# A fused convolution, attention and expert kernel: roots moved from GpSimd to VectorE, stores made steps of SyncE's order, PSUM banks shared out anew

## The chip, the cores and the metric

The kernel runs on one core of one Trainium2 chip. The metric is the device time of one execution in microseconds. The core's engines run their own instruction streams in order: TensorE (PE in the profile), VectorE (DVE), ScalarE (ACT), GpSimd (POOL) and SyncE (SP), which only issues DMAs here. An instruction whose inputs are not ready holds up everything behind it on its engine.

## The reference, cut to what matters

The input `x` is 32 images of 128 channels by 56 by 56 pixels, float32. Two layers are applied.

```python
# layer 0: 3x3 convolution of signs, with a residual
x = x + conv(sign(group_norm(x)), sign(w)) * Alpha
# layer 1: tokens, one per pixel (3136 per image, 128 wide)
t = tokens(x)
n = layer_norm(t)
q, k, v = n @ Wq + bq, n @ Wk + bk, n @ Wv + bv
t = t + q * sum_over_tokens(k * v)
# experts: each token goes to its best 2 of 8
n = layer_norm(t)
p = softmax(n @ router_w + router_b)
top_p, top_i = top_k(p, 2);  top_p = top_p / sum(top_p)
t = t + sum_k top_p[k] * (n @ expert_w[top_i[k]] + expert_b[top_i[k]])
```

`w` is made of M, Z and rv; only its sign is used. Each layer norm needs a reciprocal square root per token, `1/sqrt(var + eps)`, and so two per token in all.

## The kernel before, in words

An image is a tile `x` of 128 channels by 3136 pixels. Its tokens are 25 chunks of up to 128 rows. The work of an image runs through these stages:

- **Convolution.** `conv` makes nine bfloat16 matmuls for eight rows of the image into a PSUM bank (tag `mm`, line 534). `conv_add` on VectorE adds them to x. `to_tokens` turns chunks (tag `tr`).
- **First norm.** VectorE takes statistics per chunk (line 574), `var1` makes 25 variances per partition (lines 443 to 446), and `rstd1` makes their reciprocal roots `r1`. ScalarE scales the tokens by r1 (`scaled`, line 625), and TensorE makes their Gram matrix (`gram`, line 634), from which the eight `kv_` steps derive the sum over k times v. `project` and `project_out` (lines 749 and 763) form q and the router's inputs. `project_add` adds them to the tokens and takes the second statistics.
- **Second norm and routing.** `var2` and `rstd2` make `r2`. `route_1` (lines 836 to 838) to `route_5` on VectorE find the two experts of each token and their gates.
- **Dense experts.** For the first 12 chunks of images 0 to 27, and for all 25 of images 28 to 31, every expert is computed. `gate_turn`, `gate_out` and `gate_parts` turn the gates and store them in DRAM (`gp`, `gb`). `spread` loads them back broadcast over partitions (`bc` and `gt`). `gated` multiplies tokens with the gates of two experts on VectorE (line 1010), and `experts` accumulates eight experts' products of a block of 512 tokens in one PSUM bank (tag `ff`, lines 1022 and 1028). `finish` adds the sum to the tokens (line 1039) and issues the store to the output (line 1040).
- **Sorted experts.** The other 13 chunks of images 0 to 27 are sorted by their pair of experts. The images form groups of 8, 8, 8 and 4. `pair_of`, `places` and `row_numbers` find where each token goes. `row_add` and `scatter` write its row to `rows` in DRAM by an indirect DMA on GpSimd (line 1201), 13 per image. When a group is complete, `list_1` to `list_4` make a list of tiles of 128 rows with one pair each. `tile_load` reads four tiles (a quad) from DRAM (`t_in`), `tile_turn` and `tile_turned` transpose them, `tile_experts` multiplies two tiles at a time with their two experts (tag `to`, line 1476), `tile_first` and `tile_second` weigh and add the products (ScalarE line 1491, VectorE line 1503). `tile_out` adds the tokens (line 1518) and stores the quad into `res` (line 1520). There are 116 quads. `result_rows` computes each token's row in `res` (`res_no`, line 1266), and `gather` fetches 13 chunks per image back by indirect DMAs (line 1271, tile `back`). `back_turn` and `back_out` turn and copy them, and the store to the output follows (line 1295).

**What sets the order.** The whole program is first a list of steps. `at` gives each step a due time, an engine, an estimate of its work in microseconds, the steps that it comes after, rings of buffers that it takes or frees, and a `delay` between the end of its work and the time when others may use what it made. `in_order` (line 94) is a planner: it plays the engines through with these estimates and picks, among the steps that can start within `AHEAD` of the earliest, the one that is due first. The order that it finds is the order in which the instructions are issued; the estimates change nothing else. `ROOM` holds the number of buffers in each ring as the planner counts them, and the `bufs` of the tile pools are those that exist. A step's `do` may issue instructions on several engines. In the kernel before, stores are issued inside steps of VectorE or ScalarE (`finish`, `tile_out`, `back_out`, `gate_out`, `gate_parts`); the DMA then stands in SyncE's queue at the place of that step, and the planner doesn't count it as SyncE's work.

**GpSimd's queue.** All scatters and gathers are issued there, at most two under way at a time (`in_turn`, `IN_FLIGHT`). The reciprocal roots stand in the same queue: `rstd_of` (line 449) raises the 25 variances per partition to the power −0.5 in one GpSimd instruction at line 450, 64 times in all. The planner counts it as 4.5 us with a delay of 3.0 (rstd1) or 6.0 us (rstd2).

**PSUM.** There are eight banks: `mm` 2, `tr` 2, `acc` 1, `ff` 1 and `to` 2. The bank `to` also serves `places`, `list_sum` and `list_3`.

Of the kernel before, what the change touches and what calls it, by code (L numbers as in the profile page):

```python
# [54 lines left out]
C = 128  # L55
# [3 lines left out]
N_EXP = 8  # L59
# [10 lines left out]
GROUPS = (8, 8, 8, 4)  # L70
IN_FLIGHT = 2
TILE_PACE = (0.7, 0.6, 0.4, 0.3)
# [9 lines left out]
    x=3, tok=3, mm=2, tr=2, acc=1, ff=1, to=2, y=3, qs=3, tt=4, bc=4, gt=2, gated=2,  # L82
    t_in=3, turned=2, v=3, back=6, sent=2,
# [13 lines left out]
def in_order(steps):  # L97
# [29 lines left out]
    while len(order) < len(steps):  # L127
# [19 lines left out]
        for f in followers.get(s.key, []):  # L147
            missing[f.key] -= 1
            same = f.engine == s.engine
            f.ready = max(f.ready, clock[s.engine] if same else s.done + HOP[f.engine])  # L150
            if not missing[f.key]:
                waiting.setdefault(f.engine, []).append(f)
# [4 lines left out]
def conv_attn_moe_kernel(  # L157
# [56 lines left out]
    ps_ff = ctx.enter_context(tc.tile_pool(name="ps_ff", bufs=1, space=PSUM))  # L214
    ps_to = ctx.enter_context(tc.tile_pool(name="ps_to", bufs=2, space=PSUM))
# [8 lines left out]
    m_half = const.tile([C, 1], F32, name="m_half")  # L224
    nc.vector.memset(m_half, -0.5)
# [223 lines left out]
    def rstd_of(var, dst):  # L449
        nc.gpsimd.tensor_tensor(dst, var, m_half.to_broadcast([C, n_ck]), ALU.pow)  # L450
# [4 lines left out]
    def plan_image(i: int):  # L455
# [160 lines left out]
        at(s + 44, ("rstd1", i), "POOL", 4.5, rstd1, after=[("var1", i)], delay=3.0)  # L616
# [289 lines left out]
        def gate_out():  # L906
# [12 lines left out]
            nc.scalar.copy(d["parts"][:, :, 0, :], d["gt"])  # L919
            gp = dpool.tile([n_gb, N_EXP, WIDE], F32, tag="gp", name=f"gp_{i}")  # L920
            nc.sync.dma_start(
                gp.rearrange("(h b) e (c t) -> (b e c) h t", h=per_j, c=PER), sb[:rows]
# [3 lines left out]
        def gate_parts():  # L926
# [6 lines left out]
            nc.vector.tensor_sub(parts[:, :, 2, :], rem, parts[:, :, 1, :])  # L933
            gb = dpool.tile([n_db, 3, N_EXP, WIDE], BF16, tag="gb", name=f"gb_{i}")
# [17 lines left out]
        at(s + 119, ("rstd2", i), "POOL", 4.5, rstd2, after=[("var2", i)], delay=6.0)  # L952
# [15 lines left out]
            after=[("gate_turn", i), ("gate_parts", i - 1), ("spread", i - 2, n_units - 1)],  # L968
            delay=3.0,
# [3 lines left out]
            after=[("gate_out", i)], free=[("tr", ("gate_turn", i))], delay=4.0,  # L973
# [62 lines left out]
        def finish(b):  # L1036
            lo, hi = cols_of(b)
            t = d.pop(("tt", b))[:, : hi - lo]
            nc.vector.tensor_add(t, t, d.pop(("ff", b))[:, : hi - lo])
# [3 lines left out]
        last_unit = (last_dense(i - 1) + 1) * pairs - 1  # L1043
# [599 lines left out]
```

## Time and profile before

| | |
|---|---|
| device time, median of 3 runs | 3037.72 us (3020.0 to 3044.76) |
| the profiled execution | 3027.72 us |
| its span, first to last instruction | 3026.0 us |
| mean granted TensorE clock | 0.879 |
| TensorE busy | 2332.3 us (77%) |
| VectorE busy | 1975.5 us (65%) |
| ScalarE busy | 1352.9 us (45%) |
| GpSimd busy | 1151.2 us (38%), of which the 64 roots 281.9, the 364 scatters 445.3 and the 364 gathers 414.4 |
| DMA | 467.06 MB, 154 GB/s on average |

A profile page lists busy time per engine, groups of instructions by source line, and waits: `A <- B: sum, times, longest` is the idle time of engine A just before an instruction, ended by the named instruction of B. A timeline row gives start, duration, engine, line, operation, output and input, how many instructions the row merges, and in brackets the idle time before it and what ended it. A view of stretches gives the busy time of each engine between two times; PEclk is the TensorE clock that was granted, as a share of full speed. The scatters of images 0 to 13 are issued before the first gather at 1084.0 us, those of images 14 to 27 after it; the last scatter is issued at 2510.7 us and the last gather at 3018.9 us.

### The profile page before, as it was taken

The page shows a single profiled execution, that of the slowest core. Times are in us where ns is not written, and L with a number is a line of the kernel's source. Part 1 is how long each engine was busy: PE and PEld are TensorE (multiplying, and loading weights), DVE is VectorE, ACT ScalarE, POOL GpSimd, SP SyncE. Part 2 cuts the span into 40 slices and gives each one's busy share as a digit, 9 for nine tenths or more (in the row PEclk, how much of TensorE's full clock was granted, in tenths as well). Part 3 has the DMA queues.
Part 4 walks back from the last instruction along what each step waited for, and adds up shares of the span by engine and source line. Part 5 has one row for each costly group of instructions (what it writes and reads, how often), then busy time and mean ns, then how long its engine had stood idle before and what let it go on. Part 6 is the DMA issues. An engine that isn't in the chain of part 4 may idle for free. (4 is left out here: it accounts for less than half of the span.)

```text
span 3026.0 us, 43562 instructions
## 1 busy us (share of the span) xinstructions
PE 2332.3 (77%) x11990; PEld 1535.9 (51%) x11990; DVE 1975.5 (65%) x5998; ACT 1352.9 (45%) x4211; POOL 1151.2 (38%) x908
## 2 busy tenths in 40 slices
PE   5887978798888986677678767767686687869767
PEld 3654545455666654354455444545464454645533
DVE  3867867687777876576566656557565574657644
ACT  5545544455555554344544443434444443432310
POOL 1244333333332344423343345443433433234443
PEclk9888989899999998898889888888797798979878
DMA  3343444355555544463545344334664464746556
GB/s 128 98 148 132 163 132 135 133 176 177 168 174 162 180 147 144 122 191 120 163 145 176 116 140 156 104 123 153 185 179 116 141 177 121 232 126 225 172 186 209
DMA packets 309729, 467.06 MB, mean 154 GB/s; under 512 B 61129, under 2 KB 209009, under 8 KB 309490
## 3 DMA queue, kind: packets, MB, share of 16 engines
q1 hardware_dynamic: 285186, 414.11, 43.1%
q0 software_dynamic: 23296, 46.64, 5.1%
q10 hardware_dynamic: 1008, 3.54, 0.3%
q8 instruction: 100, 1.64, 0.2%
q14 instruction: 139, 1.14, 0.1%
HBM read 345.73 MB, written 118.39 MB: 153 GB/s over the span
## 5 line engine op out<-in xcount | busy, mean ns | idle before, releaser
L1028 PE MATMUL ff<-gated,ew_d 128*128 128x512 f32 (+1 forms) x1792 | 902.8, 639 | 189.9 <-DVE gated L1010 189.7
L1201 POOL DMA_INDIRECT rows<-tok,row_no x364 | 445.3, 1223 | 882.4 <-issue 320.8
L1271 POOL DMA_INDIRECT back<-res,res_no x364 | 414.4, 1138 | 786.5 <-PE back_ps L1286 392.4
L1028 PEld LDWEIGHTS ff<-gated,ew_d 128*128 128x128 f32 x1792 | 351.5, 210 | 594.5 <-issue 341.1
L1010 DVE TENSOR_TENSOR gated<-tt,bc 128x1024 f32<-128x1024 f32 (+1 forms) x448 | 527.5, 1183 | 145.0 <-PE ff L1028 105.5
L534 PE MATMUL cv<-xs,w_bin 128*128 128x448 bf16 x2016 | 437.1, 363 | 35.4 <-ACT xs L500 18.6
L625 ACT ACTIVATE y<-tok,r 128x128 f32<-128x128 f32 (+1 forms) x800 | 256.5, 396 | 397.2 <-POOL r L450 374.5
L450 POOL TENSOR_TENSOR r<-var,m_half 128x25 f32<-128x25 f32 x64 | 281.9, 4410 | 199.1 <-DVE var L446 183.0
L763 ACT ACTIVATE qs<-q,r 128x136 f32<-128x136 f32 (+1 forms) x800 | 244.2, 386 | 206.1 <-PE q L749 175.9
L1476 PE MATMUL to<-ew_s,turned 128*128 x1856 | 265.2, 290 | 85.2 <-ACT turned L1464 39.8
L534 PEld LDWEIGHTS <-w_bin 128*128 128x128 bf16 x2016 | 199.9, 100 | 220.9 <-issue 74.4
L1476 PEld LDWEIGHTS to<-ew_s,turned 128*128 128x128 f32 x1856 | 243.6, 202 | 123.6 <-ACT turned L1464 58.2
L749 PE MATMUL q<-move,x 128*128 128x144 f32 (+1 forms) x1600 | 261.5, 304 | 22.6 <-ACT qs L767 11.1
L749 PEld LDWEIGHTS q<-move,x 128*128 128x128 f32 (+1 forms) x1600 | 230.0, 200 | 70.8 <-issue 34.6
L1491 ACT ACTIVATE v<-to,t_in 128x128 f32<-128x128 f32 x464 | 186.0, 457 | 174.3 <-PE to L1476 145.0
L634 PE MATMUL gram<-y 128*128 128x129 f32 (+1 forms) x1600 | 218.7, 286 | 39.8 <-ACT y L625 39.6
L634 PEld LDWEIGHTS gram<-y 128*128 128x128 f32 (+1 forms) x1600 | 205.3, 199 | 73.0 <-ACT y L625 45.1
L1503 DVE SCALAR_TENSOR_TENSOR v<-to,t_in,v 128x128 f32<-128x128 f32 x464 | 139.4, 343 | 126.6 <-ACT v L1491 108.9
L574 DVE BATCH_NORM_STATS2 st<-tok 128x6 f32<-128x128 f32 (+1 forms) x800 | 177.6, 276 | 24.8 <-ACT tok L567 23.7
L775 DVE TENSOR_TENSOR tok<-tok,qs 128x384 f32<-128x384 f32 (+1 forms) x288 | 148.6, 516 | 58.4 <-ACT qs L763 33.4
L782 DVE BATCH_NORM_STATS2 st<-tok 128x6 f32<-128x128 f32 (+1 forms) x800 | 181.5, 276 | 0.0
L545 DVE SCALAR_TENSOR_TENSOR x<-cv,alpha_col,x 128x448 f32<-128x448 f32 x224 | 151.0, 675 | 42.8 <-PE cv L534 36.7
(208 smaller groups left out, 2733.0 us busy)
## 6 DMA issues: line engine op xcount, KB each, us to landing
bc<-gp SPq DMA_DIRECT2D x432, 512.0 KB
x<-in_x_dram SPq DMA_DIRECT2D x64, 784.0 KB
t_in<-rows SPq DMA_DIRECT2D x464, 66.0 KB
res<-v SPq DMA_DIRECT2D x116, 256.0 KB
out_dram<-tt SPq DMA_DIRECT2D x108, 256.0 KB
out_dram<-o SPq DMA_DIRECT2D x84, 256.0 KB
gt<-gb SPq DMA_DIRECT2D x324, 24.0 KB
rows<-zeros SPq DMA_DIRECT2D x116, 66.0 KB
```

What stands on the lines that cost most here:

```text
L450: nc.gpsimd.tensor_tensor(dst, var, m_half.to_broadcast([C, n_ck]), ALU.pow)
L534: nc.tensor.matmul(cv, lhsT=w_bin[:, t, :], rhs=xs[:, b * ROWS + dy : b * ROWS + dy + ROWS, dx : dx + width], start=(t == 0), stop=(t == T ...
L625: nc.scalar.mul(y[:n, j, :C], d["tok"][:n, c, :C], d["r1"][:n, c : c + 1])
L634: nc.tensor.matmul(d["gram"], lhsT=y[:n, j, :C], rhs=y[:n, j, :], start=(c == 0), stop=(c == n_ck - 1),)
L749: nc.tensor.matmul(p[:n, k, :], lhsT=d["x"][:, c * C : c * C + n], rhs=move, start=True, stop=True,)
L763: nc.scalar.mul(qs[:n, k, : C + N_EXP], p[:n, k, : C + N_EXP], d["r1"][:n, c : c + 1])
L1010: nc.vector.tensor_tensor(g[:, :, :n], d["tt", b][:, :n].unsqueeze(1).to_broadcast([C, 2, n]), d.pop(("bc", b, k))[:, :, :n], ALU.mult,)
L1028: nc.tensor.matmul(d["ff", b][:, :n], lhsT=ew_d[:, e * C : (e + 1) * C], rhs=g[:, j, :n], start=False, stop=(e == N_EXP - 1),)
L1201: dma = nc.gpsimd.indirect_dma_start(out=groups[group]["rows"], out_offset=bass.IndirectOffsetOnAxis(ap=d["row_no"][:n, c - N_DENSE : c - ...
L1271: dma = nc.gpsimd.indirect_dma_start(out=d["back", c][:n, :], out_offset=None, in_=groups[group]["res"][: quads_of(group) * WIDE, :], in_o ...
L1476: nc.tensor.matmul(p[:, k, j, :], lhsT=t[:, n * C : (n + 1) * C], rhs=ew_s[:, bass.ds(d["cols", q][j][n], C)], start=True, stop=True,)
L1491: nc.scalar.activation(d["v", q][:, 2 * h + k, :], d["to", q, h][:, k, 0, :], AF.Identity, bias=row[:, C + 2 : C + 3], scale=row[:, C : C ...
```

## The change

It has four parts.

1. **Roots.** `rstd_of` no longer uses GpSimd. VectorE makes a first guess from the bits of the variance (a shift right by one and a subtraction from 0x5F3759DF, both on int32) and improves it in three Newton steps of three instructions each: 11 instructions on 25 columns in place of one. The steps rstd1 and rstd2 become VectorE steps of 1.25 us without delay.
2. **Stores.** The stores inside `finish`, `tile_out`, `back_out`, `gate_out` and `gate_parts` become steps of SyncE of their own (`store`, `tile_store`, `back_store`, `gate_store`, `parts_store`), with places in SyncE's order, work and landing times. The buffers that they read are freed by them. `spread`, `tile_load`, `pad` and `gather` get larger estimates of work or landing time, and a step on the same engine as one with a delay now waits in the plan for the landing, unless it is of the same kind. `gather` comes after `tile_store`, and `spread` after `gate_store`.
3. **Buffers.** The row numbers `row_no` and `res_no` get four buffers instead of two, and `result_rows` of an image comes after the gathers of the image three before it, instead of two. `back` gets eight buffers instead of six, while the planner still counts six.
4. **PSUM.** `ff` gets two banks and `to` one.

```diff
 ROOM = dict(
-    x=3, tok=3, mm=2, tr=2, acc=1, ff=1, to=2, y=3, qs=3, tt=4, bc=4, gt=2, gated=2,
-    t_in=3, turned=2, v=3, back=6, sent=2,
+    x=3, tok=3, mm=2, tr=2, acc=1, ff=2, to=1, y=3, qs=3, tt=4, bc=4, gt=2, gated=2,
+    t_in=3, turned=2, v=3, back=6, sent=2, o=2,
 )
...
+GATE_LANDS, SPREAD_LANDS, STORE_LANDS, TILE_LANDS, GATHER_LANDS = 5.0, 6.5, 5.0, 6.0, 6.0
...
-            same = f.engine == s.engine
+            same = f.engine == s.engine and (not s.delay or f.key[0] == s.key[0])
...
-    ps_ff = ctx.enter_context(tc.tile_pool(name="ps_ff", bufs=1, space=PSUM))
-    ps_to = ctx.enter_context(tc.tile_pool(name="ps_to", bufs=2, space=PSUM))
+    ps_ff = ctx.enter_context(tc.tile_pool(name="ps_ff", bufs=2, space=PSUM))
+    ps_to = ctx.enter_context(tc.tile_pool(name="ps_to", bufs=1, space=PSUM))
...
     def rstd_of(var, dst):
-        nc.gpsimd.tensor_tensor(dst, var, m_half.to_broadcast([C, n_ck]), ALU.pow)
+        square = spool.tile([C, n_ck], F32, tag="square", bufs=1, name="square")
+        shape = [C, n_ck]
+        nc.vector.tensor_tensor(
+            square.bitcast(I32),
+            var.bitcast(I32),
+            one_i.to_broadcast(shape),
+            ALU.logical_shift_right,
+        )
+        nc.vector.tensor_tensor(
+            dst.bitcast(I32), guess.to_broadcast(shape), square.bitcast(I32), ALU.subtract
+        )
+        for _ in range(NEWTON):
+            nc.vector.tensor_mul(square, dst, dst)
+            nc.vector.scalar_tensor_tensor(square, square, -0.5, var, ALU.mult, ALU.mult)
+            nc.vector.scalar_tensor_tensor(dst, square, 1.5, dst, ALU.add, ALU.mult)
...
-        at(s + 44, ("rstd1", i), "POOL", 4.5, rstd1, after=[("var1", i)], delay=3.0)
+        at(s + 44, ("rstd1", i), "DVE", 1.25, rstd1, after=[("var1", i)])
...
-        at(s + 119, ("rstd2", i), "POOL", 4.5, rstd2, after=[("var2", i)], delay=6.0)
+        at(s + 119, ("rstd2", i), "DVE", 1.25, rstd2, after=[("var2", i)])
...
+        at(
+            s + 138, ("gate_store", i), "SP", 0.4, gate_store,
+            after=[("gate_out", i), ("spread", i - 2, last_units(i - 2))], delay=GATE_LANDS,
+        )
...
+        at(
+            s + 139, ("parts_store", i), "SP", 0.35 * n_db, parts_store,
+            after=[("gate_parts", i), ("spread", i - 2, last_units(i - 2))], delay=GATE_LANDS,
+        )
...
-                    begin + n * unit - 12, ("spread", i, n), "SP", 0.1 + 0.3 * (k == 0), spread, b, k,
-                    after=[("gate_out", i), ("spread", i, n - 1), ("spread", i - 1, last_unit)]
-                    + ([("gate_parts", i)] if k == 0 else []),
-                    take=["bc"] if k else ["bc", "gt"], delay=4.5,
+                    begin + n * unit - 12, ("spread", i, n), "SP", 0.35 + 1.0 * (k == 0), spread, b, k,
+                    after=[("gate_store", i), ("spread", i, n - 1), ("spread", i - 1, last_unit)]
+                    + ([("parts_store", i)] if k == 0 else []),
+                    take=["bc"] if k else ["bc", "gt"], delay=SPREAD_LANDS,
...
-                free=[("ff", ("experts", i, b * pairs)), ("tt", ("tt_turn", i, b))],
+                free=[("ff", ("experts", i, b * pairs))],
+            )
+            at(
+                begin + n * unit + 5, ("store", i, b), "SP", 0.35, store, b,
+                after=[("finish", i, b)], free=[("tt", ("tt_turn", i, b))], delay=STORE_LANDS,
             )
...
-            d["res_no"] = spool.tile([C, n_sort], U32, tag="res_no", bufs=2, name=f"res_no_{i}")
+            d["res_no"] = spool.tile([C, n_sort], U32, tag="res_no", bufs=4, name=f"res_no_{i}")
...
-            d["back", c] = bpool.tile([C, C], F32, tag="back", bufs=6, name=f"back_{i}_{c}")
+            d["back", c] = bpool.tile([C, C], F32, tag="back", bufs=8, name=f"back_{i}_{c}")
...
-            after=[("list_2", group), ("gather", i - 2, n_ck - 1), ("result_rows", i - 1)],
+            after=[("list_2", group), ("gather", i - 3, n_ck - 1), ("result_rows", i - 1)],
+            delay=3.0,
...
-                    + [("tile_out", group, q) for q in range(quads_of(group))],
-                    take=["back"], delay=3.0,
+                    + [("tile_store", group, q) for q in range(quads_of(group))],
+                    take=["back"], delay=GATHER_LANDS,
...
+            at(
+                due + each * k / n_sort + 8, ("back_store", i, b), "SP", 0.35, back_store, b,
+                after=[("back_out", i, b)], free=[("o", ("back_out", i, b))], delay=STORE_LANDS,
+            )
...
+            at(
+                due + 8, ("tile_store", g, q), "SP", 0.35, tile_store, g, q,
+                after=[("tile_out", g, q), ("tile_store", g, q - 1)]
+                + ([("gather", last_of[g - 2], n_ck - 1)] if q == 0 and g > 1 else []),
+                free=[("v", ("tile_first", g, q, 0))], delay=STORE_LANDS,
             )
```

## The prediction

> **What bounds the kernel now.** I read the summary, the waits, the stages and one stretch of the timeline, in that order. The summary says that no engine is full:
>
> ```profile
> span 3026.0 us, 43562 instructions
> PE 2332.3 (77%) x11990; PEld 1535.9 (51%) x11990; DVE 1975.5 (65%) x5998; ACT 1352.9 (45%) x4211; POOL 1151.2 (38%) x908
> ```
>
> TensorE stands idle for about 690 us. The waits of all engines say what the others stood at:
>
> ```profile
> POOL back L1271 <- PE back_ps L1286: 392.4, 70, 38.9
> ACT y L625 <- POOL r L450: 374.5, 29, 30.5
> ...
> DVE logit L837 <- POOL r L450: 236.1, 28, 26.4
> ...
> DVE res_no L1266 <- DMA back<-res,res_no: 162.2, 15, 24.1
> ...
> PE ff L1022 <- DVE tt L1039: 68.4, 14, 14.4
> ...
> DVE a L1181 <- POOL r L450: 57.4, 4, 19.1
> ```
>
> Three of these are the reciprocal root on GpSimd (L450), awaited by ScalarE and VectorE for 374.5 + 236.1 + 57.4 = 668 us, though 64 of them are busy for only 282 us. The stages show when it hurts:
>
> ```profile
> 640.00:1084.00 444.00, 402.19 (x2286) 276.92 (x2285) 355.47 (x1107) 254.54 (x802) 145.22 (x89) 0.95 0.55 171
> 1084.00:1600.00 516.00, 372.85 (x1974) 246.92 (x1974) 326.04 (x1037) 236.86 (x749) 210.59 (x150) 0.85 0.48 150
> ```
>
> The columns are the stretch, its length, busy time of PE, PE loads, DVE, ACT and POOL, granted clock, DMA share and GB/s. The first gather starts at 1084.0. Before it TensorE is busy 402/444 = 91%, after it 373/516 = 72%. The timeline from 1249 on shows how; first GpSimd, then the engines that wait for it:
>
> ```profile
> 1270.29 0.95 POOL L1271 DMA_INDIRECT back<-res,res_no  x1 [0.89 <-DMA back<-res,res_no]
> 1271.68 0.95 POOL L1271 DMA_INDIRECT back<-res,res_no  x1 [0.44 <-issue]
> 1272.65 8.64 POOL L450 TENSOR_TENSOR r<-var,m_half 128x25 f32<-128x25 f32 x2
> ```
>
> ```profile
> 1257.04 0.18 DVE L446 SCALAR_TENSOR_TENSOR var<-var,diff 128x25 f32<-128x25 f32 x1
> ...
> 1277.04 0.70 ACT L625 ACTIVATE y<-tok,r 128x128 f32<-128x128 f32 x2 [26.95 <-POOL r L450]
> 1277.50 1.23 PE L634 MATMUL gram<-y 128*128 128x129 f32 x4 [17.93 <-ACT y L625]
> 1281.32 0.37 DVE L837 TENSOR_TENSOR logit<-logit,r 128x200 f32<-128x200 f32 x1 [23.79 <-POOL r L450]
> ```
>
> The variances are ready at 1257.2; GpSimd takes up the two roots at 1272.65, behind gathers and scatters queued ahead of them, and the whole core waits. Pairing each variance (L446) with its root (L450), the time from one to the other is 5.4 us on average in 640 to 1084 and 13.8 us in 1084 to 1600, at most 28.1 us. Laying TensorE's gaps over the stretches in which ScalarE or VectorE waits for r gives 347 us of TensorE idle; with VectorE's waits for an old gather (res_no) added it is 381 us, with the ff wait 401 us. This overlap, not the 668 us, is what can come back.
>
> **What the Trainium skill says.** "GPSIMD Engine Reference", section 3.1: an elementwise operation on two inputs is about twice as slow on GpSimd as on VectorE at 2048 elements. The trace agrees in direction, and more: pow over 25 columns takes 4.41 us, a VectorE operation of that shape 0.17 to 0.19 us (L443 to L446). "VectorE: DVE Perf Modes", errata section: an f32 tensor-tensor takes (N+151)/0.96 ns, so 183 ns for N = 25; L443 has 188. "TensorE: Matmul & The Clock Gate", Part 1: TensorE falls to half clock after some 3.4 us idle. The trace agrees: granted clock is 0.95 in the busy stage, 0.85 after. "Perfetto Trace Analysis", section on tensor performance: independent groups of matmuls should rotate through PSUM banks so that emptying one overlaps the next. The 68.4 us before L1022 show the lack of it for ff; the change takes the same thing from `to`.
>
> **The change, part by part.**
>
> *Roots by Newton on VectorE.* Removed: 64 × 4.41 = 282 us of GpSimd, its place in that queue and two hops between engines. Added: per root 2 + 3 × 3 = 11 instructions of 25 columns. The shift isn't in the trace; it is bounded by the shortest and longest row of that shape, 0.17 and 0.19 us, and I take 0.18 (at most 1.3 us over all 64 either way). So 11 × 0.18 = 2.0 us busy and, each depending on the last (dependent ones start 0.20 us apart at 1207.2), 2.2 us from var to r instead of 4.4 plus the queue. In sum 64 × 2.0 = 127 us more VectorE. It lies beside TensorE's work where VectorE has room (880 busy of 1426 us from 1084 to 2510, 62%), less so in 640 to 1084 (80%). Behind it on VectorE stand gated products that feed ff. I count a quarter, +32; bounds 0 and +127. The gain: of 381 us I count 70%, −267. The rest goes to what is late next: `PE back_ps <- DMA back` is 95 us now, and gathers keep their own queue. Bounds −150 and −381.
>
> *Clock.* Filling gaps warms TensorE. After 1084 it is busy 1425 us at 0.85 to 0.86; halfway to 0.95 is 0.90, and 1425 × (1 − 0.85/0.90) = 79 us. Half of that shows in the span: −40; bounds 0 and −79.
>
> *More buffers for row numbers, back 6 to 8.* The res_no wait is within the 381. `back` gets two buffers that the planner (still 6) doesn't count on; that shields GpSimd's 392 us at L1271, of which only 84 us coincide with TensorE idle. No root is behind it any more, so I count nothing; at most −84, and where the cover of other GpSimd work goes, nothing is lost either, since a buffer adds no work.
>
> *Stores as SyncE steps.* The same DMAs: 112 tt, 112 o, 116 res, 32 gp and 112 gb, about 0.35 us of issue each on SP. They are moved later in SP's order, past bc and t_in loads. SP stands long at them (L1520 257 us, L1295 97 us), but who needs the loads behind hardly waits: gated for bc 9.3 us, PE turn for t_in 8.9, ACT v 5.6. So −10, bounds −25 and +30. The loss: the tt, o and v buffers are freed by a store that now may sit behind loads, and a tile_store that comes late holds back every gather of its group. A gate_store or parts_store now delays spread by 5.0 + 0.5 us in the plan only. The dearer SP costs and landing times (spread 6.5, gather 6.0) shift order, not work.
>
> *PSUM.* ff 1 to 2: takes the 68.4 us before L1022, of which 20 are outside the 381: −20; bounds 0 and −68. `to` 2 to 1: each of 232 half tiles (L1476) must be emptied by two L1491 (2 × 0.457) and two L1503 (2 × 0.343 us), 1.6 us plus hops, before the next may start; places, list_sum and list_3 take the same bank. Now TensorE waits 29.5 us for L1503 here. The plan puts other matmuls between as long as ScalarE and VectorE keep time: a quad comes every (1080−675)/32 = 12.7 us for the first group, and two emptyings with matmuls need about 7. Cover gone, the cost is 232 × 1.6 = 371 us. I take +40; bounds 0 and +371.
>
> Sum against the profiled execution, 3027.7 us (span 3026.0 and 1.7 around it): −267 −40 −10 −20 +32 +40 = −265, so 2763. The median of the runs, 3037.7, is 0.33% above the profiled one: **2770 us**.
>
> **Rivals.**
>
> *The pace before the gathers returns (2600).* Images' scatters come 74 us apart in 640 to 1084 and about 103 apart from 1084 to 2510 (14 images). If nothing takes the root's place, the latter falls to about 78: 14 × 25 = 350 saved, and some 70 of the last 516 us: 3027.7 − 420 = 2608. For it: all the work is in both stages but 13 gathers an image. Against: those need GpSimd too.
>
> *The indirect DMAs remain the pace (2900).* From 1084 on there are 364 gathers and 182 scatters, two under way at most, now 3.56 us apart. In the last 166 us 63 go at 2.6 us with little else queued. If in the mix they only reach 3.3, 546 × 3.3 = 1802 after a start at about 1070, and 20 for the end: about 2890. For it: `POOL rows <- DMA rows` 190.8 us, and the last chain runs through gathers. Against: most of those waits have no compute behind them once the root is gone.
>
> *The single `to` bank decides (3150, slower).* If ScalarE or VectorE is behind plan, TensorE, being in order, stands at L1476, and all behind it: ff, conv, back. Gain without it is 305 us, so it decides from 305/232 = 1.3 us per half tile. At 1.9 us it costs 441: 3027.7 − 305 + 441 = 3164. For it: the planner prices L1491 at 0.70 per half where two take 0.91, and L1503 at 0.53 where two take 0.69. Against: its hops, 0.5 to 0.8 us, exceed the trace's 0.1 to 0.2, so the plan has slack.
>
> *The change does not do what it says* (the roots still late, as VectorE is itself behind gathers): about 3010.
>
> **Numbers.** 2770 (2680 to 2860): 0.50. The early pace: 0.20. The gather pace: 0.15. Within 1%: 0.04. The single bank: 0.11. Differences under 1% can't be told from none here (the three runs span 0.8%). The range of 8 in 10 goes from 2580 to 2960: it leaves out the slower case, no change, and a twentieth below. Faster by over 1% is 0.85, within 1% 0.04, slower 0.11.
>
> **What would show it.** Right: no L450 on POOL; VectorE busy some 2100 us; the waits for r gone from ACT y and DVE logit; from the first gather on TensorE over 80% busy at a clock near 0.90; `PE ff <- DVE tt` near zero; waits at L1476 below 70 us. Wrong: L1476's waits for DVE v in hundreds of microseconds (single bank); `PE back_ps <- DMA back` far above 95 us (gather pace); gated waiting for bc or tiles for t_in by far more than 9 us (stores).

## The result and the profile after

The changed kernel takes **2550.05 us** (median of 4 runs, 2532.56 to 2556.39); the kernel before, beside it, 3036.92 us. The ratio is 0.8394, 95% interval 0.8339 to 0.8448: faster by 16%. The prediction was 2770 us with a range of 2580 to 2960; the direction was right, the measured time lies 30 us below the range, and the gain is almost twice the forecast one. The profiled execution took 2551.04 us, 477 less than that of before.

The summary of the page after, span, busy times and granted clock (busy time in us, share of the span):

```profile
span 2549.3 us, 44202 instructions
PE 2244.8 (88%) x11990; PEld 1490.2 (58%) x11990; DVE 2058.0 (81%) x6703; ACT 1349.8 (53%) x4211; POOL 885.7 (35%) x844
...
PEclk9999999999999999989999999979999999999986
```

TensorE has the same 11990 matmuls. It is busy 87 us less, as its mean granted clock rose from 0.879 to 0.956, and span minus busy time fell from 693.7 to 304.5 us: 389 us of idle are gone. 389 + 87 = 476 us, the whole gain. VectorE has 705 instructions and 82.5 us more.

The waits of all engines after (sum in us, times, longest):

```profile
ACT v L1549 <- PE to L1534: 282.0, 151, 7.1
...
POOL back L1319 <- PE back_ps L1334: 152.5, 59, 12.1
...
PE back_ps L1334 <- DMA back<-res,res_no: 121.4, 53, 11.2
...
DVE gated L1050 <- PE ff L1068: 96.1, 61, 13.3
...
ACT y L650 <- DVE r L471: 44.9, 10, 10.9
...
PE to L1534 <- DVE v L1561: 40.2, 32, 2.9
...
DVE res_no L1314 <- DMA back<-res,res_no: 26.2, 6, 7.8
```

The 668 us in which ScalarE and VectorE waited for a root on GpSimd are 44.9 us, all ScalarE's. The wait for an old gather (`res_no`) went from 162.2 to 26.2, GpSimd's wait for a free `back` from 392.4 to 152.5. The wait of `ff` for VectorE's additions (68.4 before) is in no row. TensorE's largest wait before was for the gated products of VectorE, which itself stood waiting for roots:

```profile
PE ff L1028 <- DVE gated L1010: 189.7, 31, 25.3
```

The same wait (`PE ff L1068`) is 15.2 us after. What waits now is mostly ScalarE for `to`, which costs no TensorE time (the run with the old PSUM banks below).

To see where the 477 us came from, both runs are cut at the same points of the work: the first scatter of image 1, the first scatter of image 8, the first gather, the last scatter, the end. The views of stretches have the same columns as in the prediction. Before:

```profile
0.00:192.50 192.50, 134.91 (x704) 89.96 (x704) 111.50 (x392) 103.48 (x318) 46.31 (x134) 0.90 0.32 109
192.50:677.90 485.40, 403.99 (x2000) 249.12 (x1999) 360.69 (x1163) 238.96 (x788) 182.26 (x106) 0.91 0.45 150
677.90:1084.00 406.10, 368.24 (x2107) 255.12 (x2106) 328.31 (x1018) 233.83 (x735) 138.61 (x87) 0.95 0.56 170
1084.00:2510.70 1426.70, 1034.74 (x5504) 700.50 (x5504) 880.73 (x2755) 632.38 (x1961) 579.71 (x426) 0.85 0.47 147
2510.70:3026.00 515.30, 390.47 (x1684) 241.19 (x1682) 294.29 (x675) 144.30 (x411) 204.27 (x158) 0.86 0.58 184
```

After:

```profile
0.00:165.40 165.40, 124.09 (x686) 81.20 (x687) 113.68 (x439) 104.00 (x320) 26.49 (x130) 0.97 0.37 127
165.40:559.10 393.70, 384.64 (x1993) 243.74 (x1992) 380.78 (x1318) 237.52 (x783) 126.64 (x92) 1.00 0.57 184
559.10:956.40 397.30, 367.46 (x2143) 256.79 (x2141) 349.68 (x1143) 237.59 (x744) 103.27 (x79) 1.00 0.57 174
956.40:2106.60 1150.20, 1015.35 (x5627) 692.76 (x5626) 940.28 (x3144) 642.07 (x2006) 468.67 (x397) 0.95 0.61 188
2106.60:2549.30 442.70, 353.26 (x1549) 215.68 (x1547) 273.56 (x661) 128.61 (x364) 160.65 (x149) 0.89 0.65 200
```

By length the five stages gained 27, 92, 9, 277 and 73 us. The fourth, with scatters and gathers mixed, is the largest, as expected. The second is the surprise: before any gather, images 1 to 8 had 81 us of TensorE idle and have 9 now. An image took 69 us there and takes 56 (393.7/7), and VectorE is now 97% busy (380.78/393.70): it, and not TensorE alone, is full in this stage.

One root in the fourth stage, on VectorE (start, duration, line, operation; rows of VectorE alone):

```profile
1493.47 0.18 DVE L452 SCALAR_TENSOR_TENSOR var<-var,diff 128x25 f32<-128x25 f32 x1
...
1493.86 0.17 DVE L459 TENSOR_TENSOR square<-var,one_i 128x25 int32<-128x25 int32 x1
1493.94 0.28 DVE L807 BATCH_NORM_STATS2 st<-tok 128x6 f32<-128x128 f32 x1
1494.15 0.17 DVE L465 TENSOR_TENSOR r<-guess,square 128x25 int32<-128x25 int32 x1
...
1496.71 0.19 DVE L471 SCALAR_TENSOR_TENSOR r<-square,r 128x25 f32<-128x25 f32 x1
```

The root is done 3.3 us after its variance. Between its instructions stand those of other steps: within one engine the program isn't issued step by step, as the section on the kernel before says, but with independent neighbours mixed in. This matters below. Pairing all 64 variances with their roots, the time from one to the other is 5.5 us on average and 14.7 at most, where the kernel before had 10.5 and 28.1.

### The profile page after: what moved, and what is told of

The parts are those of the page before. It is cut to its first block, busy times and chain, and to the rows that moved or that the text cites. A ratio compares the mean times of both kernels' runs of the same rounds, so it can differ in the third digit from the quotient of the medians.

```text
span 2549.3 us, 44202 instructions
## 1 busy us (share of the span) xinstructions
PE 2244.8 (88%) x11990; PEld 1490.2 (58%) x11990; DVE 2058.0 (81%) x6703; ACT 1349.8 (53%) x4211; POOL 885.7 (35%) x844
## 5 line engine op out<-in xcount | busy, mean ns | idle before, releaser
L1068 PE MATMUL ff<-gated,ew_d 128*128 128x512 f32 (+1 forms) x1792 | 848.2, 599 | 15.3 <-DVE gated L1050 15.2
L1249 POOL DMA_INDIRECT rows<-tok,row_no x364 | 466.6, 1282 | 1060.4 <-DMA rows<-tok,row_no 155.9
L1319 POOL DMA_INDIRECT back<-res,res_no x364 | 409.6, 1125 | 596.4 <-PE back_ps L1334 152.5
L1068 PEld LDWEIGHTS ff<-gated,ew_d 128*128 128x128 f32 x1792 | 320.6, 196 | 271.0 <-issue 212.7
L1534 PE MATMUL to<-ew_s,turned 128*128 x1856 | 264.9, 283 | 88.0 <-DVE v L1561 40.2
L559 PEld LDWEIGHTS <-w_bin 128*128 128x128 bf16 x2016 | 199.1, 100 | 187.3 <-issue 44.9
L650 ACT ACTIVATE y<-tok,r 128x128 f32<-128x128 f32 (+1 forms) x800 | 247.2, 395 | 46.4 <-DVE r L471 44.9
L774 PE MATMUL q<-move,x 128*128 128x144 f32 (+1 forms) x1600 | 252.4, 296 | 13.8 <-DVE x L570 7.9
L774 PEld LDWEIGHTS q<-move,x 128*128 128x128 f32 (+1 forms) x1600 | 221.9, 194 | 50.8 <-issue 28.8
L659 PEld LDWEIGHTS gram<-y 128*128 128x128 f32 (+1 forms) x1600 | 213.9, 200 | 55.0 <-ACT y L650 29.6
L659 PE MATMUL gram<-y 128*128 128x129 f32 (+1 forms) x1600 | 228.5, 290 | 13.1 <-ACT y L650 12.8
L599 DVE BATCH_NORM_STATS2 st<-tok 128x6 f32<-128x128 f32 (+1 forms) x800 | 180.4, 276 | 21.9 <-ACT tok L592 21.6
L807 DVE BATCH_NORM_STATS2 st<-tok 128x6 f32<-128x128 f32 (+1 forms) x800 | 184.8, 276 | 0.0
L1334 PE MATMUL back_ps<-ident,back 128*128 128x128 f32 (+1 forms) x364 | 75.7, 299 | 123.3 <-DMA back<-res,res_no 121.4
```

The lines of the kernel that those rows point to most:

```text
L559: nc.tensor.matmul(cv, lhsT=w_bin[:, t, :], rhs=xs[:, b * ROWS + dy : b * ROWS + dy + ROWS, dx : dx + width], start=(t == 0), stop=(t == T ...
L650: nc.scalar.mul(y[:n, j, :C], d["tok"][:n, c, :C], d["r1"][:n, c : c + 1])
L659: nc.tensor.matmul(d["gram"], lhsT=y[:n, j, :C], rhs=y[:n, j, :], start=(c == 0), stop=(c == n_ck - 1),)
L774: nc.tensor.matmul(p[:n, k, :], lhsT=d["x"][:, c * C : c * C + n], rhs=move, start=True, stop=True,)
L807: nc.vector.bn_stats(st2[:n, c, :], d["tok"][:n, c, :C])
L1068: nc.tensor.matmul(d["ff", b][:, :n], lhsT=ew_d[:, e * C : (e + 1) * C], rhs=g[:, j, :n], start=False, stop=(e == N_EXP - 1),)
```

## Experiments

The theory was: the roots came late since they stood in GpSimd's queue behind scatters and gathers that wait for their turn. The rivals for the gain: the stores and estimates (a different plan), the PSUM banks, and the buffers. All runs, with medians of four executions and the ratio to the kernel before beside them (its medians lie between 3024 and 3037):

| run | median us | ratio (95%) |
|---|---|---|
| the change | 2550.05 | 0.8394 (0.8339 to 0.8448) |
| roots_alone | 2605.90 | 0.8612 (0.8593 to 0.8631) |
| roots_undone | 2998.71 | 0.9905 (0.9876 to 0.9935) |
| stores_undone | 2553.50 | 0.8452 (0.8430 to 0.8474) |
| psum_undone | 2545.78 | 0.8396 (0.8355 to 0.8437) |
| bufs_undone | 2629.40 | 0.8671 (0.8624 to 0.8718) |
| roots_bufs | 2564.81 | 0.8464 (0.8421 to 0.8507) |
| roots_old_plan | 2714.48 | 0.8964 (0.8917 to 0.9012) |
| before_flight4 | 2863.21 | 0.9482 (0.9436 to 0.9527) |
| newton8 | 2708.57 | 0.8944 (0.8902 to 0.8986) |
| spare15 | 2553.81 | 0.8468 (0.8426 to 0.8510) |
| newton2 | 2537.65 | 0.8391 (0.8356 to 0.8426) |
| in_flight4 | 2428.11 | 0.8025 (0.7987 to 0.8063) |
| flight3 | 2534.15 | 0.8376 (0.8341 to 0.8412) |
| flight8 | 2622.58 | 0.8662 (0.8603 to 0.8721) |
| flight4_newton2 | 2586.73 | 0.8567 (0.8535 to 0.8599) |
| flight4_spare15 | 2655.28 | 0.8743 (0.8690 to 0.8796) |

### Which part does it

**The roots alone, in the kernel before.**

```diff
-        nc.gpsimd.tensor_tensor(dst, var, m_half.to_broadcast([C, n_ck]), ALU.pow)
+        # the 11 VectorE instructions of the change
...
-        at(s + 44, ("rstd1", i), "POOL", 4.5, rstd1, after=[("var1", i)], delay=3.0)
+        at(s + 44, ("rstd1", i), "DVE", 1.25, rstd1, after=[("var1", i)])
...
-        at(s + 119, ("rstd2", i), "POOL", 4.5, rstd2, after=[("var2", i)], delay=6.0)
+        at(s + 119, ("rstd2", i), "DVE", 1.25, rstd2, after=[("var2", i)])
```

> The kernel before with one part of the change: the roots by Newton steps on VectorE, stores, buffers and PSUM as before. Theory (the root behind gathers and scatters in GpSimd's queue is the cost): most of the 487 us come, 2630 to 2750 us. Rival 1 (the stores in SyncE's order and the dearer landing times made the plan true to the chip, and that is the gain): little, 2900 to 3000 us. Rival 2 (PSUM: two ff banks): 2900 to 3000 us as well, with the wait of ff for DVE tt still tens of us.

It gains 418 us of the 487, with nothing else of the change in it.

**The change with its roots back on GpSimd** (the same lines the other way round).

> The changed kernel with the roots back on GpSimd as one power instruction, 4.5 us with delays of 3.0 and 6.0 in the plan, all else as changed. Theory: 2850 to 3000 us, with the waits of ACT y and DVE logit for r back at several hundred us. Rival 1 (stores and estimates): stays near the changed kernel, 2560 to 2700 us. Rival 2 (PSUM): the same, 2560 to 2700 us.

Three parts without the roots gain 1%. Its waits show the roots as late as ever, 722 us against 668 in the kernel before, and the single bank holding TensorE (`PE to`, 128 us) once ScalarE and VectorE fall behind:

```profile
ACT y L632 <- POOL r L453: 383.3, 31, 29.7
...
DVE logit L844 <- POOL r L453: 288.5, 29, 30.0
...
PE to L1516 <- DVE v L1543: 128.1, 41, 22.1
...
DVE a L1211 <- POOL r L453: 50.6, 3, 19.8
```

**The stores and estimates of before, with roots, buffers and banks of the change.** The edit is part 2 of the diff, taken out:

```diff
-            at(
-                begin + n * unit + 5, ("store", i, b), "SP", 0.35, store, b,
-                after=[("finish", i, b)], free=[("tt", ("tt_turn", i, b))], delay=STORE_LANDS,
-            )
...
```

> The changed kernel with the stores back inside the steps that make their data and the old estimates of work and landing, with Newton roots, buffers and PSUM as changed. Theory: a small loss, 2560 to 2640 us, since those who need loads hardly waited for them. Rival 1: most of the gain goes, 2800 us or more, with SyncE standing at stores and gated products waiting for bc.

2553.5 against 2550.1 us: the intervals of the two ratios overlap. The stores and estimates are worth nothing that can be told apart, in either direction.

**The PSUM banks of before.**

```diff
-    x=3, tok=3, mm=2, tr=2, acc=1, ff=2, to=1, y=3, qs=3, tt=4, bc=4, gt=2, gated=2,
+    x=3, tok=3, mm=2, tr=2, acc=1, ff=1, to=2, y=3, qs=3, tt=4, bc=4, gt=2, gated=2,
...
-    ps_ff = ctx.enter_context(tc.tile_pool(name="ps_ff", bufs=2, space=PSUM))
-    ps_to = ctx.enter_context(tc.tile_pool(name="ps_to", bufs=1, space=PSUM))
+    ps_ff = ctx.enter_context(tc.tile_pool(name="ps_ff", bufs=1, space=PSUM))
+    ps_to = ctx.enter_context(tc.tile_pool(name="ps_to", bufs=2, space=PSUM))
```

> The changed kernel with one ff bank and two to banks, all else as changed. Theory: within 40 us of the changed kernel either way, 2520 to 2590 us: the ff wait of 68 us comes back in part, and the waits at the to matmuls (88 us) go in part. Rival 2: most of the gain goes, 2700 us or more.

2545.8 us: nothing either, for the two banks together; the run doesn't part a gain by `ff` from a loss by `to`. With the second bank back, ScalarE's wait for `to` falls from 282 to 115 us and the time stays, so that wait wasn't on the path.

**The buffers of before, in the changed kernel.**

```diff
-            d["row_no"] = spool.tile([C, n_sort], U32, tag="row_no", bufs=4, name=f"row_no_{i}")
+            d["row_no"] = spool.tile([C, n_sort], U32, tag="row_no", bufs=2, name=f"row_no_{i}")
...
-            d["res_no"] = spool.tile([C, n_sort], U32, tag="res_no", bufs=4, name=f"res_no_{i}")
+            d["res_no"] = spool.tile([C, n_sort], U32, tag="res_no", bufs=2, name=f"res_no_{i}")
...
-            d["back", c] = bpool.tile([C, C], F32, tag="back", bufs=8, name=f"back_{i}_{c}")
+            d["back", c] = bpool.tile([C, C], F32, tag="back", bufs=6, name=f"back_{i}_{c}")
...
-            after=[("list_2", group), ("gather", i - 3, n_ck - 1), ("result_rows", i - 1)],
+            after=[("list_2", group), ("gather", i - 2, n_ck - 1), ("result_rows", i - 1)],
```

> The changed kernel with two buffers for row_no and res_no, six for back, and result_rows after the gathers of the image two before. The roots alone stand at 2606 us, the whole at 2550; stores undone and PSUM undone each left it at about 2550. If the buffers carry the rest: 2580 to 2620 us, with the wait of res_no for DMA back at 100 us or more. If the rest is shared by overlapping parts: 2540 to 2575 us.

79 us slower than the change. VectorE's wait for `res_no` is 76.6 us again (26.2), GpSimd's for `back` 286.3 (152.5), TensorE's for VectorE at `to` 77.6 (40.2). Which of the three sizes does it, or the image that `result_rows` waits for, wasn't separated.

**Roots and buffers alone, in the kernel before** (the two edits above together).

> The kernel before with two parts of the change, the roots and the buffers; stores and PSUM as before. If these two are the whole gain: 2530 to 2575 us. If stores and PSUM, which each may stand in for the other, carry something together: 2580 to 2610 us.

2564.8 us: the buffers add 41 to the roots' 418, and what is left for stores and banks together is some 15 us, not told apart from none. So the two undoings (449 and 79) and the two additions (418 and 41) agree in kind: roots first, buffers second, nothing else that can be told apart.

### Why the root's place costs so much

**Only the root's instructions changed, the plan left as it was.** The planner goes on treating rstd1 and rstd2 as GpSimd's work of 4.5 us with 3 or 6 us of delay; only the body of `rstd_of` is new.

```diff
-        nc.gpsimd.tensor_tensor(dst, var, m_half.to_broadcast([C, n_ck]), ALU.pow)
+        # the 11 VectorE instructions of the change; both at(...) as before
```

> The kernel before with only the instructions of the root replaced by Newton on VectorE; the plan still counts the roots as GpSimd steps of 4.5 us with delays of 3.0 and 6.0, so that every step stands where it stood before. Theory A (the chip's own GpSimd queue made the roots late): nearly as fast as the kernel with the roots moved in the plan too (2606 us), 2600 to 2720 us. Theory B (the plan, which made room for a slow root, was what cost): most of the 418 us stay, 2850 to 3020 us.

313 us of the gain come with the plan untouched, so from what happens on the chip. Another 109 come when the plan knows it (2714 to 2606). In this run the roots cost ScalarE 99 us, and the wait for `res_no` is as long as before:

```profile
DVE res_no L1284 <- DMA back<-res,res_no: 181.6, 17, 24.0
...
ACT y L643 <- DVE r L468: 99.2, 17, 14.5
```

There is a rival here. In the kernel before, GpSimd also stood 183.0 us for variances (`POOL r L450 <- DVE var L446`) and was busy 282 us with the roots, and the gathers behind it had to wait; without roots in its queue they could come sooner, and that could be the gain. But TensorE's wait for gathered rows was too short for that, and it didn't fall. Before, and then in this run:

```profile
PE back_ps L1286 <- DMA back<-res,res_no: 95.4, 39, 10.0
```

```profile
PE back_ps L1304 <- DMA back<-res,res_no: 143.7, 56, 11.1
```

The wait for `res_no` rose too (162.2 before). What fell is the part of TensorE's idle time that coincides with waits for r: laid over each other as in the prediction, 347 us before, 34 here, 9 with the roots alone and 8 in the changed kernel. So it is the wait for the root, and not the gathers behind it, that carries the 313 us.

**Four indirect DMAs under way in the kernel before,** its roots still on GpSimd, so that its queue drains sooner:

```diff
-IN_FLIGHT = 2
+IN_FLIGHT = 4
```

> The kernel before with four indirect DMAs under way instead of two, roots still on GpSimd, all else as before. Theory (the roots stand behind gathers and scatters that wait for a DMA two before them): GpSimd's queue drains sooner, the roots come sooner, 2750 to 2930 us, with the waits of ACT y and DVE logit for r well below 668 us. If the roots are late for other reasons, such as gathers waiting for a free back buffer: 2950 to 3030 us.

161 us faster by a constant alone. From variance to root it is 6.1 us on average now (10.5 with two), and the waits for r are 352 us in place of 668:

```profile
ACT y L625 <- POOL r L450: 179.3, 27, 19.9
DVE logit L837 <- POOL r L450: 159.4, 28, 15.5
...
DVE a L1181 <- POOL r L450: 13.1, 2, 9.2
```

This speaks for the queue theory without touching the root, and GpSimd is as busy with the roots as before. TensorE's idle time that coincides with waits for r fell from 347 to 138 us. It isn't pure: gathers also come sooner (`PE back_ps` waits 33.3 us for them, 95 before).

**Eight Newton steps in place of three,** 15 more instructions in a chain; the plan still counts 1.25 us.

```diff
-NEWTON = 3
+NEWTON = 8
```

> The changed kernel with eight Newton steps instead of three, the plan unaware of it: 26 instructions, some 5.2 us from variance to root, more than the 4.4 us of the power on GpSimd, and 64 x 15 x 0.18 = 173 us more VectorE. Theory A (the wait in the queue, not the duration of the root): 2590 to 2700 us, the added VectorE work showing by a quarter to three quarters. Rival C (the root's duration on the path): 64 x 3 us = 190 us or more on top of the added work, 2740 us or more.

158.5 us slower than the change. VectorE's busy time rose by 143.5 us to 2201.5, which looks like the price. The next run tests that.

**The same 15 instructions, on nobody's path.**

```diff
         for _ in range(NEWTON):
...
+        spare = spool.tile([C, n_ck], F32, tag="spare", bufs=1, name="spare")
+        for _ in range(5):
+            nc.vector.tensor_mul(spare, var, var)
+            nc.vector.scalar_tensor_tensor(spare, spare, -0.5, var, ALU.mult, ALU.mult)
+            nc.vector.scalar_tensor_tensor(spare, spare, 1.5, spare, ALU.add, ALU.mult)
```

> The changed kernel with 15 more VectorE instructions of 25 columns behind each root, whose result nobody reads, the plan unaware: the added work of eight Newton steps without the longer way from variance to root for ScalarE. Eight steps cost 158 us. If VectorE's busy time is what they cost: 2680 to 2730 us, as with eight steps. If the longer way to the root (15 x 0.2 = 3 us, 64 times) is: 2550 to 2620 us.

2553.8 us: 960 more instructions cost nothing that can be told apart. The timeline shows where they go:

```profile
204.77 0.18 DVE L469 TENSOR_TENSOR square<-r 128x25 f32<-128x25 f32 x1
204.87 0.18 DVE L474 TENSOR_TENSOR spare<-var 128x25 f32<-128x25 f32 x1
204.99 0.19 DVE L470 SCALAR_TENSOR_TENSOR square<-square,var 128x25 f32<-128x25 f32 x1
205.09 0.18 DVE L475 SCALAR_TENSOR_TENSOR spare<-spare,var 128x25 f32<-128x25 f32 x1
205.21 0.19 DVE L471 SCALAR_TENSOR_TENSOR r<-square,r 128x25 f32<-128x25 f32 x1
```

L469, L470 and L471 depend on each other and start 0.22 us apart; a spare one fits between two of them. In the changed kernel the same chain stands alone, at the same pace:

```profile
205.55 0.19 DVE L469 TENSOR_TENSOR square<-r 128x25 f32<-128x25 f32 x1
205.77 0.18 DVE L470 SCALAR_TENSOR_TENSOR square<-square,var 128x25 f32<-128x25 f32 x1
205.99 0.19 DVE L471 SCALAR_TENSOR_TENSOR r<-square,r 128x25 f32<-128x25 f32 x1
```

So newton8's loss doesn't come from the number of VectorE's instructions. It isn't shown that busy time is free, though: a stretch in which two instructions overlap counts once, and so the spare ones added 59.6 us of busy time where the chain added 143.5. The summaries of newton8 and then of spare15 (2058.0 us of VectorE in the change):

```profile
PE 2323.2 (86%) x11990; PEld 1533.3 (57%) x11990; DVE 2201.5 (81%) x7663; ACT 1363.9 (50%) x4211; POOL 904.4 (33%) x844
```

```profile
PE 2244.7 (88%) x11990; PEld 1489.6 (58%) x11990; DVE 2117.6 (83%) x7663; ACT 1351.5 (53%) x4211; POOL 886.4 (35%) x844
```

From variance to root it takes 15.3 us on average in newton8 (5.9 with the spare ones), and ScalarE waits 100.6 us for r (44.9 in the change). But TensorE doesn't stand idle in those waits: they coincide with its idle time for 7 us, against 8 in the change. Its idle time as a whole grew by 82 us, and its waits for results of VectorE from 119 to 203 us; the other 78 us are its busy time, at a granted clock of 0.932 in place of 0.956. So the chain seems to cost by holding up VectorE's own stream, and with it what TensorE awaits from there, and not by ScalarE's wait for r. No run separates the two.

This also corrects the theory. 15.3 us is more than the 10.5 of the kernel before, which took 3037 us and not 2709. How late a root is doesn't give its cost; what the other engines stand for it does: newton8's chain lies in VectorE's own stream, with other work mixed in, and its r is awaited for 100.6 us; GpSimd's root came late behind waits for DMAs and was awaited for 668.

**Two Newton steps.**

```diff
-NEWTON = 3
+NEWTON = 2
```

> The changed kernel with two Newton steps, a root that is exact to some 5e-6 only: eight dependent instructions where the change has eleven. Five steps more cost 158 us, 10.5 us for each instruction added to the chain (64 roots). If the chain of the root is exposed on both sides of three steps: 3 x 10.5 = 32 us less than 2550, 2505 to 2530 us. If it is exposed only where it is long: 2540 to 2560 us. If the order of the program that comes out by chance outweighs it: outside both, above 2560 us.

2537.7 us, 12 less (ratio 0.8391 against 0.8394: not told apart). At its present length the chain costs nothing that can be told apart.

### What bounds it next

**Four under way in the changed kernel** (the `IN_FLIGHT` edit above).

> The changed kernel with four indirect DMAs under way instead of two. If the gathers' pace still bounds the end (PE back_ps waits 121 us for DMA back, the last 200 us have TensorE at 70%): 2450 to 2520 us. If the pace is set by GpSimd's own work or by the DMA engines: within 1% of 2550 us.

2428.1 us, 122 less than the change and 20% less than the kernel before: **the version that beats both**. TensorE is busy 91% of the span at a clock of 0.976, and it hardly waits for gathers any more (121.4 before this edit):

```profile
span 2422.7 us, 44157 instructions
PE 2216.3 (91%) x11990; PEld 1479.2 (61%) x11990; DVE 2056.7 (85%) x6703; ACT 1347.8 (56%) x4211; POOL 907.2 (37%) x844
```

```profile
PE back_ps L1334 <- DMA back<-res,res_no: 30.3, 23, 8.0
```

The gain lies after the first gather, as the theory of the gathers' pace has it: from there to the end it takes 1465.6 us in place of 1592.9, and up to there the same as the change to within 1 us.

**Three, and eight.**

```diff
-IN_FLIGHT = 2
+IN_FLIGHT = 3
```

> The changed kernel with three indirect DMAs under way. If the pace of the gathers bounds the end and eases in step with the number: 2450 to 2510 us. If the number matters little and four hit a lucky order: 2530 to 2560 us.

> The changed kernel with eight indirect DMAs under way. Four took it to 2428 us, with PE back_ps waiting 30 us for DMA back. More should bring little: 2400 to 2430 us; above 2440 us if the DMAs take one another's engines.

Three give 2534.2 us, not told apart from two (their intervals overlap), and eight 2622.6, slower than two. More isn't better, and the miss at eight raises the question whether four holds up when something small beside it changes.

**Four with two Newton steps, and four with the spare instructions,** each edit worth nothing that can be told apart by itself.

> The changed kernel with four indirect DMAs under way and two Newton steps instead of three, so a root that is exact to some 5e-6 only. If VectorE's added work shows nearly in full, as with eight steps: 64 x 3 x 0.165 = 32 us less than the 2428 us of four under way, 2385 to 2410 us. If VectorE has room again: 2415 to 2435 us.

> The changed kernel with four indirect DMAs under way and 15 spare VectorE instructions behind each root, three Newton steps. At two under way the spare ones cost nothing. If four under way hold a gain of 120 us whatever the exact order: 2415 to 2450 us. If the 2587 us with two Newton steps show that the gain hangs on the order that came out: anywhere up to 2620 us, with engines idle after the first group's lists for no releaser that the profile shows.

2586.7 and 2655.3 us: both lose the whole gain of four and more. Their traces show waits of a kind that the change and in_flight4 don't have. Of flight4_newton2, all engines:

```profile
731.16 0.96 POOL L1249 DMA_INDIRECT rows<-tok,row_no  x1 [0.30 <-issue]
731.35 0.59 ACT L592 COPY tok<-xt 128x512 f32<-128x512 f32 x1 [2.72 <-remote]
...
731.99 0.67 PE L586 MATMUL xt<-ident,x 128*128 128x128 f32 x4 [3.11 <-issue]
...
735.24 0.96 POOL L1249 DMA_INDIRECT rows<-tok,row_no  x1 [0.30 <-DMA rows<-tok,row_no]
736.37 0.59 ACT L1030 COPY tt<-l 128x512 f32<-128x512 f32 x1 [4.43 <-remote]
736.50 0.96 POOL L1249 DMA_INDIRECT rows<-tok,row_no  x1 [0.30 <-DMA rows<-tok,row_no]
737.01 1.11 PE L1516 MATMUL turn<-ident,t_in 128*128 128x128 f32 x4 [4.36 <-issue]
```

GpSimd issues scatters back to back, one each 1.26 us, and TensorE and ScalarE stand for 3 to 4 us at a time with no releaser among the core's instructions ("remote", "issue"); the matmuls at L1023 that ScalarE's L1030 reads had ended at 727.2. Of the changed kernel's variants, the waits put down to "remote" on TensorE, ScalarE and VectorE sum, over the 200 largest groups of waits of each run, to none with two under way, none in in_flight4, 104 us in flight3, 149 in flight4_newton2, 208 in flight8 and 212 in flight4_spare15, so that with three or more they rise with the time, in_flight4 apart. The kernel before with four has 98. What they are isn't settled: the bursts and the stalls stand together, and no run separates them. Nor is it shown why in_flight4 escapes; a small edit changes the order of the instructions throughout. So 2428 us holds for that one program, not for the setting.

## Why the prediction was right and wrong

**The bound: right.** That the late roots cost the time, and not GpSimd's busy 282 us, is shown by before_flight4, which keeps the 282 us and has less than half of TensorE's idle time during waits for r, and by roots_old_plan, where it goes and the waits for gathers don't. roots_alone and roots_undone show that the roots carry the gain, but not by themselves by which way.

**The step that failed: "The gain: of 381 us I count 70%, −267. The rest goes to what is late next".** The overlap of TensorE's idle with waits for r and res_no was the right measure, but nothing took its place: the overlap fell from 381 to 15 us, and TensorE's idle time as a whole by 389. With the roots alone it fell from 381 to 30, and the idle time by some 350. The heir named, `PE back_ps <- DMA back`, rose from 95 to 121 us only (166 with the roots alone). The full 381, which stood as the bound, was nearly the value; no wait in the profile was named that was large enough to carry the discount of 30%.

**Buffers, "so I count nothing": wrong.** The row-number buffers weren't priced apart from the roots, and `back`'s eight were counted at nothing. Together they are worth 41 us on top of the roots and 79 in the changed kernel. "The res_no wait is within the 381" was right as accounting, but only a part of this wait goes with the roots: with the roots alone it is still 68 us.

**Clock: right mechanism, half the size.** −40 was priced with −79 as its bound; TensorE's busy time fell by 87. The traces hold the granted clock over time, and it is either full or half. Busy time weighted with it is the same work in both, 2166 us before and 2175 after, but 333 us of busy time lay in stretches at half clock before and 140 after. Halfway to 0.95 was too little: the fourth stage reached 0.95, and busy time after the first gather, where the term was priced, fell by 57 us. The other 31 lie before it, which the sum left out: the stage of images 1 to 8 went from 0.91 to 1.00.

**Charges that didn't come: +32 for VectorE's work and +40 for the single `to` bank.** The roots added 82.5 us to VectorE's busy time and not 127, as other steps' instructions overlap with the chain. A root comes 5.5 us after its variance on average and not 2.2, for the same reason. spare15 shows that VectorE takes 59.6 us more of busy time for nothing that can be told apart, and newton2 that three instructions fewer in the chain gain nothing that can be told apart. The two bank terms, +40 for `to` and −20 for `ff`, are measured only together: psum_undone puts their sum within a few us of zero. All of TensorE's idle before that group is 88 us now (85 before), 40.2 of it for VectorE's v, against "below 70".

**ff bank −20: not visible.** The wait of `ff` for VectorE's additions is gone as forecast, but it is only 5.6 us with the old banks too (psum_undone), so that the roots took most of it along. **Stores −10: right to within the measurement.** None of the wrong signs for them came (`gated` waits 4.7 us for bc).

The idle terms summed to −225 and were −389, the clock to −40 and was −87; the two misses of 164 and 47 make up the difference between 265 and 477 us. Of the 164, 114 are the discount of 30%, 72 the two charges that didn't come, and 8 the idle time beyond the 381, less the 30 that were counted for `ff` and the stores.

**The rivals.** The early pace (2600) was the nearest. Its mechanism held for the late stage: an image takes 81 us there (1150.2/14 = 82 by length), where it said 78; before the change it was 101.5 from scatter to scatter, not the 103 that it read. It took the early pace as fixed, and that too was slowed by roots: of the 668 us, 157 lay between 140 and 640. The gather pace (2900) fell: from the first gather to the last, indirect DMAs come 2.9 us apart (1586 us for 546), and it had set 3.3. The single bank and the lack of effect fell with the runs above.

## What to carry to other kernels

A small operation in a queue of DMAs that wait for their turn can cost what its readers stand, not what it takes: pair its input with its output to find it, then lay the bottleneck's gaps over the waits for it. In this case that whole overlap was the gain in idle time; to count less, name another wait of that size, since "what is late next" needs its own number. Ask of a new chain of small instructions whether independent ones can stand between them: here 15 spare ones a root cost nothing that can be told apart, and 15 more links 158 us. And a setting that gains in one program may lose in its neighbours, as four DMAs under way did.

## What was not expected of the hardware

Dependent VectorE instructions of 25 columns start 0.22 us apart, each some 0.03 us after the end of the last; with an independent one between, starts are 0.10 to 0.12 us apart, less than the 0.18 that each lasts. The Trainium skill, "VectorE: DVE Perf Modes", says in its errata section that many small tiles pay a fixed latency per tile; the trace agrees for dependent ones only. Its section "The DRAIN you can't avoid" says that the next operation starts earlier if nothing holds it, and that is what spare15 shows. Busy time in these profiles counts an overlapping stretch once: 960 spare instructions of 0.18 us, 173 us in sum, added 59.6 us.

With three, four or eight indirect DMAs under way, other engines stood for up to 22 us (`ACT move`, flight4_newton2) with no releaser in the trace, in some programs and not in others; the cause is open.
